# Two of 32 neighbour rows read as SBUF columns by ScalarE and VectorE in place of two POOL gathers

## The chip, the cores and the metric

The kernel runs on one core of one Trainium2 chip. The metric is device time in microseconds (us) of one execution. Before the change it is 36,141.66 us, the median of three runs (36,135.79 to 36,142.94). A core has five engines with queues of their own: TensorE (PE in the profile; its weight loads are PEld), VectorE (DVE), ScalarE (ACT), GpSimd (POOL) and SyncE (SP). Data lies in HBM, in SBUF (128 partitions) and in PSUM, where TensorE writes.

## The reference

A recommender: 50,001 items have 32 near items each, and 16,384 users have a history of 100 items and a target item. First every item gets two attention vectors over its 32 near items, one from `E_in` and one from `E_out` (32 numbers each). Then each user's history rows are scored against the target row.

```python
def _neighbor_attn(E, near_full):          # E: [50001, 32]
    V = E[near_full]                       # [50001, 32, 32]
    scores = einsum('nd,nkd->nk', E, V) / sqrt(32)
    w = softmax(scores, axis=-1)
    return einsum('nk,nkd->nd', w, V)
a_sus = _neighbor_attn(E_in, near_full);  a_inf = _neighbor_attn(E_out, near_full)
h = concat([E_hist[history], a_sus[history], a_inf[history]])   # [B, 100, 128]
t = concat([E_tgt[target], a_inf[target], a_sus[target]])       # [B, 128]
z = relu(einsum('bld,hd->blh', h * t[:, None, :], W1) + b1)
exp_A = exp(einsum('blh,h->bl', z, W2[0])) * mask
attn = exp_A / sum(exp_A) ** 0.5
s = sum(h * attn);  out = sigmoid(cosine(s broadcast, t))
```

All arithmetic is float32. The indices are random, so neighbour rows and history rows lie anywhere in their tables.

## The kernel before

It has two stages, one after the other.

The **item stage** (lines 91 to 164) makes two tables in HBM, `table` and `ttab`, one row of 128 numbers per item. `egeo` in HBM holds for each item its `E_in` row and its `E_out` row side by side, 64 numbers or 256 bytes. The items, padded to 50,048, are cut into 23 blocks (`it`) of 128 partitions by 17 (`j`). One pair (it, j), 128 items, one per partition, is called a **sub-step** here; there are 391. SP loads each block's neighbour numbers `nidx`, its own rows `own` and the history embeddings into `row` (lines 101 to 107). In a sub-step POOL issues 32 indirect DMAs (line 111), one per neighbour k: each fetches 128 rows of `egeo`, one per partition, into `v[:, k]`. VectorE multiplies `v` by the own row, which ScalarE has copied to PSUM (lines 118 and 120), sums over the 32 numbers of each half (line 127), takes the maximum over the neighbours (lines 129 and 130); ScalarE makes the exponentials and their sums (line 134); VectorE takes the reciprocal (line 142), weights `v` (line 145, once per half), sums over the neighbours (line 152) and scales into `row` (line 153). ScalarE copies the two halves swapped into `trow` (line 160). At a block's end SP stores `row` and `trow` (lines 163 and 164). At the very start ScalarE's queue issues a copy of the target embeddings from HBM to HBM into `ttab` (lines 91 and 92).

Tiles come from pools with a fixed number of buffers. `v` has five, so POOL can be up to five sub-steps ahead of the engine that reads it; `prod` and `wv` have two. The order of instructions on each engine is made by the framework's scheduler from the program; waits between engines are semaphores that it places.

The **user stage** (lines 167 to 292) gathers history rows of `table` with 12,800 indirect DMAs on POOL (line 233) and target rows with 128 more (line 197), turns each on TensorE (line 246), multiplies by the target row (line 248), and runs the two matrix products (lines 255 and 265) with a ReLU between (line 257). It can begin only when the tables are complete in HBM. The last lines (295 to 325) reduce to the output.

Of the kernel before, what the change touches and what calls it, by code (L numbers as in the profile page):

```python
# [9 lines left out]

F32 = mybir.dt.float32
I32 = mybir.dt.int32
AF = mybir.ActivationFunctionType
ALU = mybir.AluOpType
AX = mybir.AxisListType

P = 128
ITEMS = 50001
K = 32
G = 32  # L20
DE = 64
D = 128
# [7 lines left out]
NSUB = 17  # L30
NITER = -(-ITEMS // (P * NSUB))
ROWS = NITER * P * NSUB

# [7 lines left out]
def kernel(  # L43
# [11 lines left out]
    out: bass.AP,  # L55
):
    nc = tc.nc

    const = ctx.enter_context(tc.tile_pool(name="const", bufs=1))
    dram = ctx.enter_context(tc.tile_pool(name="dram", bufs=1, space=bass.MemoryType.DRAM))  # L60


    table = dram.tile([ROWS, D], F32, name="table")

    ttab = dram.tile([ROWS, D], F32, name="ttab")

    ident = const.tile([P, P], F32, name="ident")
# [16 lines left out]
    scale = 1.0 / math.sqrt(G)  # L84
    near_v = near.rearrange("(i p j) k -> i p j k", p=P, j=NSUB)
    egeo_v = egeo.rearrange("(i p j) d -> i p j d", p=P, j=NSUB)
    ehist_v = ehist.rearrange("(i p j) d -> i p j d", p=P, j=NSUB)
    table_v = table.rearrange("(i p j) d -> i p j d", p=P, j=NSUB)
    ttab_v = ttab.rearrange("(i p j) d -> i p j d", p=P, j=NSUB)

    nc.scalar.dma_start(ttab[0 : ITEMS - 1, 0:DE], etgt[0 : ITEMS - 1, :])
    nc.scalar.dma_start(ttab[ITEMS - 1 : ITEMS, 0:DE], etgt[ITEMS - 1 : ITEMS, :])
    with (
        tc.tile_pool(name="n_in", bufs=2) as n_in,
        tc.tile_pool(name="n_v", bufs=5) as n_v,
        tc.tile_pool(name="n_p", bufs=2) as n_p,
        tc.tile_pool(name="n_s", bufs=3) as n_s,
        tc.tile_pool(name="n_ps", bufs=2, space=bass.MemoryType.PSUM) as n_ps,
    ):
        for it in range(NITER):  # L100
            nidx = n_in.tile([P, NSUB, K], I32, name="nidx")
            nc.sync.dma_start(nidx, near_v[it])
            own = n_in.tile([P, NSUB, 2 * G], F32, name="own")
            nc.sync.dma_start(own, egeo_v[it])
            row = n_in.tile([P, NSUB, D], F32, name="row")
            nc.sync.dma_start(row[:, :, 0:DE], ehist_v[it])
            trow = n_in.tile([P, NSUB, 2 * G], F32, name="trow")
            for j in range(NSUB):
                v = n_v.tile([P, K, 2, G], F32, name="v")
                for k in range(K):  # L110
                    nc.gpsimd.indirect_dma_start(  # L111
                        out=v[:, k].rearrange("p t d -> p (t d)"),
                        out_offset=None,
                        in_=egeo,
                        in_offset=bass.IndirectOffsetOnAxis(ap=nidx[:, j, k : k + 1], axis=0),
                    )
                own_ps = n_ps.tile([P, 1, 2 * G], F32, name="own_ps")
                nc.scalar.copy(own_ps[:, 0, :], own[:, j, :])  # L118
                prod = n_p.tile([P, K, 2, G], F32, name="prod")
                nc.vector.tensor_tensor(  # L120
                    prod.rearrange("p k t d -> p k (t d)"),
                    v.rearrange("p k t d -> p k (t d)"),
                    own_ps.to_broadcast([P, K, 2 * G]),
                    ALU.mult,
                )
                sc = n_s.tile([P, 2, K], F32, name="sc")
                nc.vector.tensor_reduce(sc.rearrange("p t k -> p k t"), prod, AX.X, ALU.add)  # L127
                top = n_s.tile([P, 2], F32, name="top")
                nc.vector.tensor_reduce(top, sc, AX.X, ALU.max)
                nc.vector.tensor_scalar(top, top, -scale, None, ALU.mult)  # L130
                ex = n_ps.tile([P, 2, K], F32, name="ex")
                tot = n_s.tile([P, 2, 1], F32, name="tot")
                for t in range(2):
                    nc.scalar.activation(  # L134
                        ex[:, t, :],
                        sc[:, t, :],
                        AF.Exp,
                        bias=top[:, t : t + 1],
                        scale=scale,
                        accum_out=tot[:, t, :],  # L140
                    )
                nc.vector.reciprocal(tot, tot)  # L142
                wv = n_p.tile([P, 2, G, K], F32, name="wv")
                for t in range(2):
                    nc.vector.tensor_tensor(  # L145
                        wv[:, t].rearrange("p d k -> p k d"),
                        v[:, :, t, :],
                        ex[:, t, :].rearrange("p (k o) -> p k o", o=1).to_broadcast([P, K, G]),
                        ALU.mult,
                    )  # L150
                att = n_s.tile([P, 2, G], F32, name="att")
                nc.vector.tensor_reduce(att, wv, AX.X, ALU.add)  # L152
                nc.vector.tensor_tensor(  # L153
                    row[:, j, DE:D].rearrange("p (t d) -> p t d", t=2),
                    att,
                    tot.to_broadcast([P, 2, G]),
                    ALU.mult,
                )
                for t in range(2):
                    nc.scalar.copy(  # L160
                        trow[:, j, t * G : (t + 1) * G], row[:, j, D - (t + 1) * G : D - t * G]
                    )
            nc.sync.dma_start(table_v[it], row)
            nc.sync.dma_start(ttab_v[it][:, :, DE:D], trow)


    num = const.tile([P, UC], F32, name="num")
# [3 lines left out]
    hist_v = history.rearrange("(p i j) l -> i p j l", p=P, j=BSUB)  # L171
    tidx = const.tile([P, UC], I32, name="tidx")
    nc.scalar.dma_start(tidx, target.rearrange("(p c) -> p c", p=P))
    tidf = const.tile([P, UC], F32, name="tidf")
    nc.vector.tensor_copy(tidf, tidx)
    with (
# [12 lines left out]
        def target_rows(c):  # L189

            if c % BSUB == 0:
                hidx = u_in.tile([P, BSUB, L], I32, name="hidx")
                nc.sync.dma_start(hidx, hist_v[c // BSUB])
# [11 lines left out]
        def target_work(c):  # L205
# [8 lines left out]
            junk = u_t.tile([P, D], F32, name="junk")  # L214
            nc.scalar.activation(junk, t, AF.Square, accum_out=tsq[:, c : c + 1])
            idf = u_s.tile([P, L], F32, name="idf")
# [11 lines left out]
        def gather(c, g):  # L228
            u = users[c]
            h = u_h.tile([P, LG, D], F32, name="h")  # L230
            for q in range(LG):
                l = g * LG + q
                nc.gpsimd.indirect_dma_start(  # L233
                    out=h[:, q, :],
                    out_offset=None,
                    in_=table,
                    in_offset=bass.IndirectOffsetOnAxis(ap=u["hidx"][:, l : l + 1], axis=0),
                )
            u["h", g] = h

        def turn(c, g):
            u = users[c]
            h = u.pop(("h", g))
            hT_ps = ps_t.tile([P, LG, P], F32, name="hT_ps")
            for q in range(LG):
                nc.tensor.transpose(hT_ps[:, q, :], h[:, q, :], ident)  # L246
            xT = u_x.tile([D, LG, P], F32, name="xT")
            nc.vector.tensor_tensor(xT, hT_ps, u["tT"].to_broadcast([D, LG, P]), ALU.mult)  # L248
            nc.vector.tensor_reduce(u["hsum"][:, g * LG : (g + 1) * LG], h, AX.X, ALU.add)  # L249
            u["xT"][g] = xT  # L250

        def hidden(c, g):
# [3 lines left out]
            z = u_x.tile([HID, LG, P], F32, name="z")  # L256
            nc.scalar.activation(z, z_ps, AF.Relu, bias=b1_sb)  # L257
            u["z"][g] = z

        def scored(c, g):  # L260
# [9 lines left out]
            ea = u_s.tile([P, L], F32, name="ea")  # L270
            nc.scalar.activation(ea, u["score"], AF.Exp)
            nc.vector.tensor_tensor(ea, ea, u["keep"], ALU.mult)
# [7 lines left out]
        for s in range(len(groups) + 2):  # L280
            if s < len(groups):
                c, g = groups[s]
# [12 lines left out]
    with (  # L295
# [3 lines left out]
        root = f_s.tile([P, UC], F32, name="root")  # L299
        nc.scalar.activation(root, den, AF.Sqrt)  # L300
        part = f_s.tile([P, UC], F32, name="part")
# [6 lines left out]
        s = f_s.tile([P, 1], F32, name="s")  # L308
# [4 lines left out]
        nc.vector.tensor_scalar(n1, n1, float(D), EPS * EPS, ALU.mult, ALU.max)  # L313
        nc.scalar.activation(n1, n1, AF.Sqrt)
        n2 = f_s.tile([P, UC], F32, name="n2")
# [65 lines left out]
```

## Time and profile before

| what | value |
|---|---|
| timed runs, median of 3 | 36,141.66 us |
| the profiled execution, its own time | 31,810.23 us |
| its span, first to last instruction | 31,808.5 us |
| last stores of the item stage issued | at 15,641 us |
| POOL busy | 24,005.7 us (75%), in 25,446 instructions |
| TensorE (PE) busy | 15,238.9 us (48%), nearly all in the user stage |
| VectorE (DVE) busy | 8,951.2 us (28%) |
| ScalarE (ACT) busy | 2,851.2 us (9%) |
| mean granted TensorE clock | 0.752 |

The profile is of one execution, and this one was 4,331 us shorter than the median of the timed runs. Register, branch and semaphore instructions, and those that only issue a DMA from SP or ScalarE, are not counted as busy; an indirect DMA on POOL is. In a row of the groups the fields are: line, engine, operation, output and input with their shapes, count, busy time in us, mean duration of one in ns, then the engine's idle time just before these instructions and what ended it; "issue" means that nothing in the profile ended it. A row of the timeline has the start in us, the duration in us, then the same names, and in brackets the idle time before it.

### The profile page before, as it was taken

To read this page: it belongs to the slowest core of one execution; us is meant where nothing else is said; L and a number is where in the kernel's file an instruction comes from. 1 tells how busy PE (TensorE), PEld (TensorE's weight loads), DVE (VectorE), ACT (ScalarE), POOL (GpSimd) and SP (SyncE) were. 2 spreads that over 40 slices of the span, in tenths; PEclk is the share of its full clock that TensorE was granted. 3 is DMA by queue.
4 is the path that set the end of the run, shared out by engine and by line. 5 is a ranking of instruction groups with operands and counts; after the bars stand their busy time and mean duration, and the time that the engine had idled before them with its cause. 6 is when DMAs were issued, how large, how long until landed. Compare 5 with 4: busy or idle time off the path is not lost.

```text
span 31808.5 us, 154035 instructions
## 1 busy us (share of the span) xinstructions
PE 15238.9 (48%) x44931; PEld 9632.2 (30%) x44931; DVE 8951.2 (28%) x10957; ACT 2851.2 (9%) x6458; POOL 24005.7 (75%) x25446
## 2 busy tenths in 40 slices
PE   0000000000000000000299999999999999999999
PEld 0000000000000000000155555555555555555555
DVE  2222222222222222222222222222222222222222
ACT  0000000000000000000011111111111111111111
POOL 7777777777777777777777777777777777777777
PEclk9999999999999999999955555555555555555555
DMA  2111111111111111111122222222222222222221
GB/s 50 30 30 30 30 31 33 30 30 30 30 34 30 30 30 30 31 33 28 37 54 53 54 53 54 53 54 54 53 54 53 54 53 54 54 53 54 53 54 52
DMA packets 981064, 1358.75 MB, mean 43 GB/s; under 512 B 559872, under 2 KB 564352, under 8 KB 977280
## 3 DMA queue, kind: packets, MB, share of 16 engines
q0 software_dynamic: 814080, 1258.87, 17.1%
q1 hardware_dynamic: 115952, 77.16, 0.9%
q10 hardware_dynamic: 50192, 12.87, 0.2%
q8 instruction: 363, 5.95, 0.1%
q14 instruction: 477, 3.91, 0.0%
HBM read 1308.76 MB, written 51.30 MB: 43 GB/s over the span
## 4 chain that ended last, share of the span: by engine, by line
POOL 49%; issue 19%; PE 15%; DMA 14%; DVE 2%; ACT 1%; POOLq 0%; ACTq 0%; SPq 0%; DVEq 0%
POOL v L111 35%; POOL h L233 13%; DMA h<-table,hidx 11%; PE z_ps L255 7%; PE score L265 5%; PE hT_ps L246 3%; DMA v<-in_egeo_dram,nidx 2%; DVE xT L248 2%; ACT z L257 1%; POOL t L197 0%; POOLq L233 0%; DVE tT L211 0%; DVE ea L274 0%; DMA nidx<-in_near_dram 0%; DMA ttab<-trow 0%
## 5 line engine op out<-in xcount | busy, mean ns | idle before, releaser
L233 POOL DMA_INDIRECT h<-table,hidx x12800 | 12079.2, 944 | 3900.9 <-issue 3159.2
L111 POOL DMA_INDIRECT v<-in_egeo_dram,nidx x12512 | 11805.1, 943 | 3820.9 <-issue 3719.2
L209 PE MATMUL hT_ps<-ident,t 128*128 128x128 f32 x128 | 53.9, 421 | 15644.7 <-DMA t<-ttab,tidx 15644.7
L265 PEld LDWEIGHTS score<-w_sb,z 128*128 128x128 f32 x25600 | 6225.7, 334 | 1080.8 <-ACT z L257 1074.0
L255 PE MATMUL z_ps<-xT,w1T 128*128 128x512 f32 x6400 | 6526.7, 1123 | 0.0
L265 PE MATMUL score<-w_sb,z 128*128 128x1 f32 x25600 | 5903.9, 335 | 235.4 <-ACT z L257 150.2
L246 PE MATMUL hT_ps<-ident,h 128*128 128x128 f32 x12800 | 4715.0, 439 | 673.3 <-DMA h<-table,hidx 520.3
L249 DVE TENSOR_REDUCE hsum<-h 128x4 f32<-128x512 f32 x3200 | 2194.7, 686 | 9243.7 <-DMA h<-table,hidx 9226.9
L209 PEld LDWEIGHTS hT_ps<-ident,t 128*128 128x128 f32 x128 | 28.8, 225 | 15644.9 <-ACT idf L217 15644.9
L246 PEld LDWEIGHTS hT_ps<-ident,h 128*128 128x128 f32 x12800 | 2676.6, 209 | 5434.3 <-issue 3257.2
L120 DVE TENSOR_TENSOR prod<-v,own_ps 128x2048 f32<-128x2048 f32 x391 | 894.6, 2288 | 10794.7 <-DMA v<-in_egeo_dram,nidx 10794.4
L257 ACT ACTIVATE z<-z_ps,b_sb 128x512 f32<-128x512 f32 x3200 | 2199.1, 687 | 13448.3 <-PE z_ps L255 13335.1
L248 DVE TENSOR_TENSOR xT<-hT_ps,tT 128x512 f32<-128x512 f32 x3200 | 2210.2, 691 | 2028.6 <-PE hT_ps L246 2026.8
L255 PEld LDWEIGHTS z_ps<-xT,w1T 128*128 128x128 f32 x6400 | 1745.4, 332 | 0.0
L145 DVE TENSOR_TENSOR wv<-v,ex 128x1024 f32<-128x1024 f32 x782 | 1398.8, 1867 | 0.0
L118 ACT COPY own_ps<-own 128x64 f32<-128x64 f32 x391 | 84.4, 216 | 11499.9 <-DVE prod L120 11498.4
L127 DVE TENSOR_REDUCE sc<-prod 128x64 f32<-128x2048 f32 x391 | 894.5, 2288 | 13.4
L152 DVE TENSOR_REDUCE att<-wv 128x64 f32<-128x2048 f32 x391 | 893.8, 2286 | 13.4
L160 ACT COPY trow<-row 128x32 f32<-128x32 f32 x782 | 131.7, 215 | 2465.7 <-DVE row L153 2465.7
L134 ACT ACTIVATE ex<-sc,top 128x32 f32<-128x32 f32 x782 | 227.7, 291 | 1081.9 <-DVE top L130 1069.2
L142 DVE RECIPROCAL tot<-tot 128x2 f32<-128x2 f32 x391 | 64.8, 166 | 362.3 <-ACT ex L134 362.3
L197 POOL DMA_INDIRECT t<-ttab,tidx x128 | 120.7, 943 | 60.5 <-issue 60.5
(49 smaller groups left out, 808.6 us busy)
## 6 DMA issues: line engine op xcount, KB each, us to landing
h<-table,hidx POOLq DMA_INDIRECT x12800, 2.5
v<-in_egeo_dram,nidx POOLq DMA_INDIRECT x12512, 2.4
table<-row SPq DMA_DIRECT2D x23, 1088.0 KB, 4.4
own<-in_egeo_dram SPq DMA_DIRECT2D x23, 544.0 KB, 3.6
row<-in_ehist_dram SPq DMA_DIRECT2D x23, 544.0 KB, 6.7
ttab<-trow SPq DMA_DIRECT2D x23, 544.0 KB, 6.8
ttab<-in_etgt_dram ACTq DMA_DIRECT2D x1, 12500.0 KB, 53.5
hidx<-in_history_dram SPq DMA_DIRECT2D x32, 200.0 KB, 2.5
```

The source lines that it names most:

```text
L111: nc.gpsimd.indirect_dma_start(out=v[:, k].rearrange("p t d -> p (t d)"), out_offset=None, in_=egeo, in_offset=bass.IndirectOffsetOnAxis(a ...
L120: nc.vector.tensor_tensor(prod.rearrange("p k t d -> p k (t d)"), v.rearrange("p k t d -> p k (t d)"), own_ps.to_broadcast([P, K, 2 * G]), ...
L127: nc.vector.tensor_reduce(sc.rearrange("p t k -> p k t"), prod, AX.X, ALU.add)
L145: nc.vector.tensor_tensor(wv[:, t].rearrange("p d k -> p k d"), v[:, :, t, :], ex[:, t, :].rearrange("p (k o) -> p k o", o=1).to_broadcast ...
L152: nc.vector.tensor_reduce(att, wv, AX.X, ALU.add)
L233: nc.gpsimd.indirect_dma_start(out=h[:, q, :], out_offset=None, in_=table, in_offset=bass.IndirectOffsetOnAxis(ap=u["hidx"][:, l : l + 1], ...
L246: nc.tensor.transpose(hT_ps[:, q, :], h[:, q, :], ident)
L248: nc.vector.tensor_tensor(xT, hT_ps, u["tT"].to_broadcast([D, LG, P]), ALU.mult)
L249: nc.vector.tensor_reduce(u["hsum"][:, g * LG : (g + 1) * LG], h, AX.X, ALU.add)
L255: nc.tensor.matmul(z_ps, w1T, u["xT"].pop(g), start=True, stop=True)
L257: nc.scalar.activation(z, z_ps, AF.Relu, bias=b1_sb)
L265: nc.tensor.matmul(u["score"][:, l : l + 1], z[:, q, :], w2_sb, start=True, stop=True)
```

## The change

In the item stage two of the 32 neighbours of each item no longer come by an indirect DMA. The `egeo` table is also held in SBUF, transposed: two items (64 numbers each) make a column of 128 numbers, one per partition, so `geoT` is 128 partitions by 25,024 columns of float32. A neighbour's two-item column is then a slice of four bytes in every partition, at an address that depends on the neighbour's number.

- **Building `geoT`** (`transposed`): 66 loads by SP of up to 384 column rows, three TensorE transposes each, and one ScalarE copy each from PSUM into `geoT`.
- **Addresses** (in `load`, once per block of 17 sub-steps): VectorE turns the last two neighbour numbers into byte addresses of columns, as floats; TensorE transposes them so that the 128 addresses of one neighbour of a sub-step lie in one row of `cols`; `odd` keeps which of the two items in the column is meant.
- **Columns** (`registers` and `columns`): an engine loads 32 addresses from `cols` into 32 of its registers with one instruction and then copies 32 columns, one instruction each, from `geoT` into the tile `g`. `AUX = ("AAAA", "DDDD")` says that ScalarE does all four blocks of 32 for one neighbour and VectorE all four for the other. For each sub-step that is four register loads and 128 copies on each of the two engines.
- **Back** (`turn`, `even`, `odd_half`): TensorE transposes the two tiles `g` into PSUM; ScalarE copies the first item of each column into `v[:, 30:32]`, and VectorE overwrites those for which `odd` is set with the second item.
- **POOL** issues 30 indirect DMAs a sub-step. `SPNUM, SPDEN = 0, 1` leaves the branch in which SP would fetch a neighbour unused.
- **Order**: the item stage's instructions on PE, ScalarE, VectorE and SP stand in the order of the program text (`manual_schedule`), as a pipeline three sub-steps deep. In step s, POOL gathers sub-step s, the column copies for s are spread in eight slots between the work on s - 1 (products, scores, exponentials) and s - 2 (weighted sums), and s - 3 is finished. `prod` and `wv` now have one buffer; `g` has two; `v` still has five.
- The stores of a block's rows (line 163 and 164 before) are issued from ScalarE's queue.

The user stage's text is the same.

```diff
+AUX = ("AAAA", "DDDD",)
+NAUX = len(AUX)
+SPNUM, SPDEN = 0, 1
+NREG = 32
+PAIRS = ROWS // 2
+NST = 3
...
+    geoT = nc.alloc_sbuf_tensor("geoT", (P, PAIRS), F32).ap()
+    geoT_at = nc.sbuf_base - 4 * PAIRS
+    geoT_b = geoT.bitcast(U8)
...
+        tc.manual_schedule(engines={E.PE, E.Activation, E.DVE, E.SP}),
+        tc.tile_pool(name="n_st", bufs=2) as n_st,
...
-        tc.tile_pool(name="n_p", bufs=2) as n_p,
+        tc.tile_pool(name="n_p", bufs=1) as n_p,
+        tc.tile_pool(name="n_g", bufs=2) as n_g,
...
+            colf = n_p.tile([P, NSUB, NAUX + 1], F32, name="colf")
+            coli = n_p.tile([P, NSUB, NAUX], I32, name="coli")
+            aux = nidx[:, :, K - NAUX : K]
+            nc.vector.tensor_scalar(coli, aux, 1, None, ALU.logical_shift_right)
+            nc.vector.tensor_copy(colf[:, :, 1 : NAUX + 1], coli)
+            nc.vector.tensor_scalar(colf[:, :, 1 : NAUX + 1], colf[:, :, 1 : NAUX + 1],
+                4.0, float(geoT_at), ALU.mult, ALU.add)
...
+            nc.tensor.transpose(col_ps[0:n, 0, :], colf.rearrange("p j a -> p (j a)"), ident)
+            cols = n_in.tile([n, P], I32, name="cols")
+            nc.vector.tensor_copy(cols, col_ps[0:n, 0, :])
...
+        def registers(s, a, engine, i0, low, top):
+            it, j = divmod(s, NSUB)
+            r = j * (NAUX + 1) + a
+            _, vals = nc.values_load_multi_w_load_instructions(
+                its[it][5][r : r + 1, i0 : i0 + NREG],
+                engines=[engine],
...
+        def columns(s, a, i0):
+            e = AUX[a][i0 // NREG]
+            vals = registers(s, a + 1, ENGINE[e], i0, geoT_at, geoT_at + 4 * (PAIRS - 1))
+            g = subs[s]["g"][a].bitcast(U8)
+            copy = nc.scalar.copy if e == "A" else nc.vector.tensor_copy
+            for i in range(i0, i0 + NREG):
+                copy(g[:, 4 * i : 4 * i + 4], geoT_b[:, ds(vals[i - i0] - geoT_at, 4)])
...
+        def turn(s):
+            back = n_pt.tile([P, 4, P], F32, name="pt")
+            for a in range(NAUX):
+                nc.tensor.transpose(back[:, a, :], subs[s]["g"][a], ident)
...
+        for s in range(NT + 3):
+            if s < NT:
+                if s % NSUB == NSUB // 2 and s // NSUB + 1 < NITER:
+                    load(s // NSUB + 1)
+                gather(s)
+            one, two, three = (0 <= s - d < NT for d in (1, 2, 3))
+            work = [
+                lambda: one and turn(s - 1),
+                lambda: (two and weighted(s - 2, 0), one and even(s - 1)),
+                lambda: two and weighted(s - 2, 1),
+                lambda: one and (odd_half(s - 1), products(s - 1)),
+                lambda: one and scores(s - 1),
+                lambda: two and attend(s - 2),
+                lambda: three and finish(s - 3),
+                lambda: one and exponents(s - 1),
+            ]
+            for w in range(len(work)):
+                work[w]()
+                if s < NT:
+                    for blocks in (acts, dves):
+                        n = len(blocks)
+                        for c in blocks[-(-w * n // 8) : -(-(w + 1) * n // 8)]:
+                            columns(s, *c)
```

## The prediction

> **What bounds the kernel now.** I read the page first, then the timeline of a stretch in the middle of the item stage, then the timeline of the hand-over to the user stage and of the first 14 us. The page's head, two rows of its busy slices, the chain and the groups of the item stage:
>
> ```profile
> span 31808.5 us, 154035 instructions
> ...
> PE   0000000000000000000299999999999999999999
> ...
> POOL 7777777777777777777777777777777777777777
> ...
> POOL v L111 35%; POOL h L233 13%; DMA h<-table,hidx 11%; PE z_ps L255 7%; PE score L265 5%; PE hT_ps L246 3%; DMA v<-in_egeo_dram,nidx 2%; DVE xT L248 2%; ACT z L257 1%; POOL t L197 0%; POOLq L233 0%; DVE tT L211 0%; DVE ea L274 0%; DMA nidx<-in_near_dram 0%; DMA ttab<-trow 0%
> ...
> L111 POOL DMA_INDIRECT v<-in_egeo_dram,nidx x12512 | 11805.1, 943 | 3820.9 <-issue 3719.2
> ...
> L120 DVE TENSOR_TENSOR prod<-v,own_ps 128x2048 f32<-128x2048 f32 x391 | 894.6, 2288 | 10794.7 <-DMA v<-in_egeo_dram,nidx 10794.4
> ```
>
> POOL is busy to the same seven tenths in every slice; the rest of its time is "issue", a gap of 0.30 us in which it waits for nothing the profile shows. So a gather costs (11805.1 + 3820.9) / 12512 = 1.249 us on POOL, and 32 of them make the 40.0 us of a sub-step (128 items; 391 of them). VectorE waits 10794 us for gathers. The timeline shows the metronome, and what VectorE and ScalarE do in between:
>
> ```profile
> 5009.04 0.94 POOL L111 DMA_INDIRECT v<-in_egeo_dram,nidx  x1 [0.30 <-issue]
> 5009.07 0.17 DVE L130 TENSOR_SCALAR top<-top 128x2 f32<-128x2 f32 x1
> ...
> 5010.17 0.17 DVE L142 RECIPROCAL tot<-tot 128x2 f32<-128x2 f32 x1 [0.93 <-ACT ex L134]
> 5010.25 3.58 DVE L145 TENSOR_TENSOR wv<-v,ex 128x1024 f32<-128x1024 f32 x2
> 5010.28 0.94 POOL L111 DMA_INDIRECT v<-in_egeo_dram,nidx  x1 [0.30 <-issue]
> ...
> 5016.44 0.34 ACT L160 COPY trow<-row 128x32 f32<-128x32 f32 x2 [6.31 <-DVE row L153]
> ```
>
> The item stage ends at 15641 us, when the last rows go to HBM; the user stage fills the other 16,160 us at the same 1.248 us a gather, with TensorE above 90% busy beside it. The built instruction streams of the user stage are the same in both kernels, engine by engine, so I leave it alone.
>
> **The two times of before.** The profiled execution took 31,810 us, the median of the timed runs is 36,142, 13.6% more. The profile cannot say where the 4,332 us lie: a gather may take 1.42 us in a timed run, or the user stage may be held by TensorE. I make the sum against 31,810, subtract the difference from 36,142, and keep the scaled saving for the low end.
>
> [...] The new VectorE copies go SBUF to SBUF with an even count[...]: L130, such an instruction, takes 168 ns at least and 187 in the mean, with up to 245 where it begins within 50 ns before a gather starts; POOL's spacing stays 1.248 us around it. [...] 10.17 to 10.25 above is 80 ns from start to start, and the two ScalarE copies of L160 (215 ns each alone) take 0.34 us together, so the second comes 125 ns after the first, of which some 25 are its 28 further elements. [...] No load of registers is in the trace of before.
>
> **The change, part by part.**
>
> Removed: 2 of 32 gathers a sub-step. 391 x 2 x 1.249 = 977 us, as POOL is the pace. The new sub-step is 30 x 1.249 = 37.5 us, and this is now the time in which each of the two other engines must do its share.
>
> ScalarE, per sub-step: 4 register loads (32 registers each), 128 column copies of 4 bytes per partition, one more copy out of PSUM (some 0.28 us, by the nearest row, L160 with 215 ns at 32 elements). Its own work stays: own_ps 0.22, the two exponentials 0.87 from first to last, trow 0.34; with the new copy 1.7 us. A column copy lies between 0.10 us (overlapped) and 0.19 (its whole duration); I take 0.10, 12.8 us. [...] I take 2.0[...]: 8.0 us. Sum 22.5 us, 15 below the pace.
>
> VectorE: own work from the rows L120, L127, L129, L130, L142, L145, L152, L153: 2.29 + 2.29 + 0.22 + 0.19 + 0.17 + 3.58 + 2.29 + 0.23 = 11.3 us, plus the predicated copy of 128x128 out of PSUM, 0.35 by the 322 ns of the three-operand instruction L220. Column copies between 0.08 and 0.166 us (L142 whole); I take 0.10: 12.8 us. Four loads at 2.0: 8.0 us. Sum 32.5 us: hidden, but with only 5 us to spare. Without that cover each further microsecond is paid 391 times. Both engines run in written order, so a load that blocks the sequencer holds up every copy and every reduction behind it; on VectorE the products, scores and weighted sums queue behind it, and POOL waits for these when its five v buffers are full.
>
> TensorE: two transposes a sub-step and one per 17, 0.45 us each, on an engine idle in this stage: nothing. The small integer preparation of addresses, 6 VectorE instructions and a copy per 17 sub-steps, about 1.5 us x 23 = 35 us in all, lies in VectorE's spare time; uncovered it would be those 35. The table stores move from SP's queue to ScalarE's, 0.33 + 0.56 us of issue per 17 sub-steps, in its spare time. SP's loads of the next 17 sub-steps are issued half-way through the present ones and stand behind nothing but the start-up loads. Instruction fetch grows: the two instruction queues moved 9.86 MB for 154,035 instructions, 64 bytes each, so 264 more are 17 KB a sub-step, on DMA engines busy 15% in this stage: nothing. The longer pipeline (three sub-steps) ends with the same chain as before, plus 0.6 us.
>
> Start-up: 66 loads of up to 196 KB, 196 transposes and 66 ScalarE copies build the transposed table before the first column can be read. ScalarE's queue is first held by the issue of the target-table copy:
>
> ```profile
> 1.39 50.72 ACTq L92 DMA_DIRECT2D ttab<-in_etgt_dram  x1
> ```
>
> So the chain starts in earnest at about 53 us. Two load buffers: a load of about 3 us (own, 544 KB, lands in 3.6) and three transposes (1.4 us) per buffer, two at a time, 2.3 us apiece: 66 x 2.3 = 150, done at about 205 us. Then sub-step 0's columns (21 us), sub-step 1 (27), and 8 us into sub-step 2 the first v buffer is free: 261 us. POOL, from 9.7 us on, has filled five buffers at 9.7 + 5 x 37.5 = 197 us. It stalls 64 us. Bounds: 15 us at 1.6 us per piece, 140 at 3.5.
>
> [...] at 0.10 us a copy the four bursts last 12.8 us and run beside 10 of the 30 gathers. Below: nothing, as around L130. Above: 0.2 us for each, 2.0 us a sub-step (once, at 15652, POOL's gap is 0.50 instead of 0.30 beside such an instruction). I take 0.05 us x 10 = 0.5 us: 391 x 0.5 = 195 us. The range keeps 0 and 780.
>
> Sum: 31,810 - 977 + 64 + 195 = 31,092, 718 us less. From the median: 36,142 - 718 = 35,424; I forecast 35,420 us.
>
> **The rivals.**
>
> VectorE becomes the bound, slower than before. Its sub-step passes the old 40.0 us when 4 loads take over 40.0 - 11.65 - 12.8 = 15.6 us, so from 3.9 us a load (122 ns a register) on. At 5 us the sub-step is 44.5, 391 x 4.5 = 1,760 us more, with start-up 37,970. [...] For: [...] copies at loaded addresses whose sequencer time the trace does not show. [...]
>
> Contention eats the gain: at 0.25 us on each of the 10 gathers, or 0.083 on all 30, 2.5 us a sub-step are back and the time is 36,142 plus 64. For: [...] the one long gap; against: L130's neighbours, undisturbed.
>
> The saving is scaled: if a gather takes 1.42 us in the timed runs, 782 x 1.42 = 1,110 us go, the other engines have 42.6 us, and with little contention the time is 35,080.
>
> **How the numbers follow.** Forecast 0.42, scaled saving 0.20, contention 0.11, VectorE bound 0.27. What a measurement of this kernel can tell is about 0.2%, 72 us. Faster: the first two, and a little of the contention case, 0.64; within: most of the contention case, 0.06; slower: 0.30. The low end is the scaled saving with a smaller start-up, 34,950. The high end goes into the VectorE case, to 4.6 us a load, 37,400, and leaves about 0.15 above it and 0.04 below. The likeliest case alone: 35,000 to 36,050.
>
> **What would show it.** Right: 30 gathers per sub-step at 1.25 to 1.28 us, the item stage ending near 14,920 us of the profiled execution, ScalarE and VectorE waiting for the gathers in every sub-step, one POOL stall before 300 us. VectorE bound: POOL waiting once per sub-step for the release of v, and VectorE's longest gaps at the register loads. Contention: POOL's spacing near 1.33 during the bursts. What would make it wrong beside these: a user stage that moves although its instructions are the same, since 4,332 us of the timed runs are unexplained.

## The result and the profile after

The changed kernel takes 38,648.35 us (median of four runs, 38,641.03 to 38,662.21), the kernel before 36,138.73 (four runs, 36,126.85 to 36,142.94). The ratio is 1.0695, interval 1.0682 to 1.0708: 2,510 us slower. The forecast was 35,420 and the top of its range 37,400.

The page of the changed kernel, its head, the chain and the groups that answer to those shown of before (the last two are the column copies):

```profile
span 38653.4 us, 262033 instructions
...
POOL 5555555555555555555556666666666666666666
...
PE 24%; another core or an unknown queue 16%; issue 4%; ACT 3%; DVE 1%; ACTq 0%; DMA 0%; DVEq 0%; POOL 0%; POOLq 0%
...
L215 POOL DMA_INDIRECT v<-in_egeo_dram,nidx x11730 | 11066.4, 943 | 8861.2 <-DVE wv L294 5394.2
...
L229 ACT COPY g<-geoT 128x4 uint8 x50048 | 5670.9, 190 | 9285.1 <-issue 8804.3
L229 DVE COPY g<-geoT 128x4 uint8 x50048 | 4645.7, 181 | 8335.7 <-issue 8098.1
```

A gather still lasts 943 ns, but POOL's row has gone from seven tenths to five, and POOL waits 5,394 us for VectorE's `wv`, that is, for a free `v` buffer. POOL has left the chain. ScalarE and VectorE now set the pace of the item stage, and they do it while idle: before their copies they wait 8,804 and 8,098 us for "issue", which is nothing that the profile shows. "Another core or an unknown queue" in the chain is time that the profile can put down to no instruction; this trace lacks many records (see what stays open).

The timeline of one sub-step of the changed kernel, where POOL restarts after its wait, and a stretch 13 us later:

```profile
5004.66 2.63 DVE L229 COPY g<-geoT 128x4 uint8 x32
5005.10 0.94 POOL L215 DMA_INDIRECT v<-in_egeo_dram,nidx  x1 [13.51 <-DVE wv L294]
...
5018.55 0.19 ACT L229 COPY g<-geoT 128x4 uint8 x1 [0.51 <-issue]
5018.55 0.17 DVE L229 COPY g<-geoT 128x4 uint8 x1 [0.53 <-issue]
5018.82 0.94 POOL L215 DMA_INDIRECT v<-in_egeo_dram,nidx  x1 [0.30 <-issue]
5019.25 0.19 ACT L229 COPY g<-geoT 128x4 uint8 x1 [0.51 <-issue]
5019.25 0.17 DVE L229 COPY g<-geoT 128x4 uint8 x1 [0.53 <-issue]
5019.95 0.19 ACT L229 COPY g<-geoT 128x4 uint8 x1 [0.50 <-issue]
...
5031.15 0.19 ACT L229 COPY g<-geoT 128x4 uint8 x1 [1.21 <-issue]
...
5032.55 0.19 ACT L229 COPY g<-geoT 128x4 uint8 x1 [1.21 <-issue]
```

At 5004.66 VectorE makes 32 copies in 2.63 us. From 5017 on, both engines start one copy at a time, at the same instants: 18.55, 19.25, 19.95; later ScalarE's start at 31.15 and 32.55. The steps are 0.70 us or a multiple of it. I call this the grid. It lasts until some 5 us after the sub-step's last gather (which starts at 5041.29), and the copies then flow again. Inside a block of 32 copies no other engine has anything to deliver: the registers are loaded (the next copy starts 0.08 us after a load's end on ScalarE, 0.09 on VectorE) and `geoT` is complete since 286 us. By start times in the whole trace, 6,435 of ScalarE's copies and 5,502 of VectorE's start 0.70, 1.40 or 2.10 us (each within 0.04) after the copy before; 99% of them lie between 3.6 and 42.2 us after the sub-step's first gather, whose last starts at 36.2.

### The profile page after: what moved, and what is told of

It reads as the page before. It is cut to its first block, busy times and chain, and to the rows that moved or that the text cites. A ratio compares the mean times of both kernels' runs of the same rounds, so it can differ in the third digit from the quotient of the medians.

```text
span 38653.4 us, 262033 instructions
## 1 busy us (share of the span) xinstructions
PE 14769.2 (38%) x45932; PEld 9639.1 (25%) x45932; DVE 13286.7 (34%) x61557; ACT 8584.7 (22%) x56963; POOL 23262.5 (60%) x24664
## 5 line engine op out<-in xcount | busy, mean ns | idle before, releaser
L215 POOL DMA_INDIRECT v<-in_egeo_dram,nidx x11730 | 11066.4, 943 | 8861.2 <-DVE wv L294 5394.2
L229 ACT COPY g<-geoT 128x4 uint8 x50048 | 5670.9, 190 | 9285.1 <-issue 8804.3
L229 DVE COPY g<-geoT 128x4 uint8 x50048 | 4645.7, 181 | 8335.7 <-issue 8098.1
L234 PE MATMUL pt<-ident,g 128*128 128x128 f32 x782 | 364.2, 472 | 18233.3 <-DVE g L229 12446.3
L460 PEld LDWEIGHTS score<-w_sb,z 128*128 128x128 f32 x25600 | 5925.4, 327 | 5409.0 <-ACT z L452 3971.5
L234 PEld LDWEIGHTS pt<-ident,g 128*128 128x128 f32 x782 | 141.7, 183 | 18451.8 <-DVE g L229 12554.3
L441 PEld LDWEIGHTS hT_ps<-ident,h 128*128 128x128 f32 x12800 | 3292.0, 261 | 3585.7 <-issue 3485.4
L441 PE MATMUL hT_ps<-ident,h 128*128 128x128 f32 x12800 | 4110.4, 424 | 6.8 <-DMA h<-table,hidx 4.7
L240 ACT COPY v<-pt 128x128 f32<-128x128 f32 x391 | 103.6, 265 | 3634.8 <-PE pt L234 3634.8
L310 DVE TENSOR_TENSOR row<-att,tot 128x64 f32<-128x64 f32 x391 | 88.3, 226 | 2019.3 <-remote 1141.0
L160 PE MATMUL pt<-ident,colf 128*51 128x128 f32 x23 | 9.8, 424 | 1175.1 <-DVE odd L157 1126.2
```

What stands on the lines that cost most here:

```text
L215: nc.gpsimd.indirect_dma_start(out=v[:, k].rearrange("p t d -> p (t d)"), out_offset=None, in_=egeo, in_offset=bass.IndirectOffsetOnAxis(a ...
L229: copy(g[:, 4 * i : 4 * i + 4], geoT_b[:, ds(vals[i - i0] - geoT_at, 4)])
L460: nc.tensor.matmul(u["score"][:, l : l + 1], z[:, q, :], w2_sb, start=True, stop=True)
```

## The experiments

**Where the 4,332 us of before are.** The profile that the prediction read was 31,810 us long, and the timed runs 36,142. So the kernel before was profiled again, unaltered.

> The kernel before, unchanged, profiled once more, to see where its timed runs (36,139 us) lose 4,330 us against its first profile (31,808 us). If ScalarE and VectorE also stall in ticks of 0.70 us here, as in the profile of the changed kernel: item stage near 15,640 us, because POOL is five buffers ahead there, and the user stage 18,500 to 20,500 us. If a gather itself is slower: spacing on POOL near 1.42 us in both stages. If the first profile was typical of profiles: 31,810 us again.

It took 36,276.74 us. Its page and its timeline in mid-stage:

```profile
span 36275.0 us, 154035 instructions
...
L111 POOL DMA_INDIRECT v<-in_egeo_dram,nidx x12512 | 13370.1, 1069 | 4124.2 <-issue 4018.5
```

```profile
5028.44 0.95 POOL L111 DMA_INDIRECT v<-in_egeo_dram,nidx  x1 [0.30 <-issue]
...
5031.07 1.10 POOL L111 DMA_INDIRECT v<-in_egeo_dram,nidx  x1 [0.30 <-issue]
5032.47 1.09 POOL L111 DMA_INDIRECT v<-in_egeo_dram,nidx  x1 [0.30 <-issue]
...
5036.67 1.79 POOL L111 DMA_INDIRECT v<-in_egeo_dram,nidx  x1 [0.30 <-issue]
5038.77 1.10 POOL L111 DMA_INDIRECT v<-in_egeo_dram,nidx  x1 [0.30 <-issue]
```

Here POOL is on the grid: gathers start 1.40 or 2.10 us apart for part of each sub-step, 1.25 elsewhere, and the mean gather is 1,069 ns instead of 943. The sub-step is 44.72 us instead of 39.93; over 391 that is 1,873 us. The user stage starts at 17,517 us instead of 15,649 and takes 18,758 us instead of 16,159. Both stages were slowed before the change, and the profile read for the prediction had none of it.

In the user stage the delay looks different. Of its 6,919 gathers between 20,000 and 30,000 us only 66 start 0.70, 1.40 or 2.10 us after the one before. There ScalarE, VectorE and POOL now and then stand for several microseconds and start again together (the product that the ScalarE line below reads was done at 25018.09):

```profile
25024.09 0.69 ACT L257 ACTIVATE z<-z_ps,b_sb 128x512 f32<-128x512 f32 x1 [9.94 <-remote]
25024.10 0.69 DVE L248 TENSOR_TENSOR xT<-hT_ps,tT 128x512 f32<-128x512 f32 x1 [8.68 <-remote]
25024.33 0.95 POOL L233 DMA_INDIRECT h<-table,hidx  x1 [3.33 <-remote]
```

"remote" says that the profile can name no instruction that ended the wait. Whether both delays have one cause is not shown.

Against this trace the changed kernel's item stage is 2,522 us longer (20,039 against 17,517) and its user stage 143 us shorter. This set of runs was 0.4% slower than the set of the result, and the 143 us belong to the set: the three kernels that follow were run in it and have user stages of 18,742 to 18,754 us. The whole loss is in the item stage.

**Which of the added instructions.** Three edits of the changed kernel, in the same set of runs.

```diff
-AUX = ("AAAA", "DDDD",)
+AUX = ("AAAA",)          # e2: ScalarE's neighbour alone, 31 gathers
+AUX = ("DDDD",)          # e3: VectorE's neighbour alone, 31 gathers
```

> Only ScalarE reads a neighbour as columns, POOL fetches 31 of 32. Theory A (the stalls come with the rate of instructions that ScalarE and VectorE together take in beside POOL's gathers): with half of the added instructions the stalls shrink to a third or less, POOL is the pace again, sub-step 38.7 us, item stage 15,200 us. Theory B (register loads and loaded addresses): the stalls per added instruction stay, ScalarE's sub-step is 40 to 48 us, item stage 15,700 to 18,800. Theory C (VectorE's copies and POOL block each other[...]): no stalls on ScalarE at all, 38.7 us.

> Only VectorE reads a neighbour as columns, POOL fetches 31 of 32. Theory A: stalls shrink to a third or less; VectorE 30 to 36 us, POOL the pace, sub-step 38.7 us, item stage 15,200 us. Theory B: VectorE stalls per added instruction as in the changed kernel, sub-step 44 to 50 us. Theory C: VectorE as in the changed kernel, sub-step 48 to 51 us, and ScalarE, which has no copies, is only late where it waits for VectorE.

e2 took 37,836 us with 48.1 us a sub-step, e3 38,401 with 49.5, against 50.5 for both together (50.9 in another set as slow as this one). Half the added instructions bring most of the delay, so it isn't proportional to them. ScalarE alone meets it too (in e2 it idles 9,327 us for "issue" before its copies, 8,804 with both), so VectorE's copies and POOL blocking each other isn't its cause.

```diff
-            vals = registers(s, a + 1, ENGINE[e], i0, geoT_at, geoT_at + 4 * (PAIRS - 1))
...
-                copy(g[:, 4 * i : 4 * i + 4], geoT_b[:, ds(vals[i - i0] - geoT_at, 4)])
+                copy(g[:, 4 * i : 4 * i + 4], geoT_b[:, 4 * (97 * i + 12000 * a) : 4 * (97 * i + 12000 * a) + 4])
```

> The changed kernel without its register loads: the same 256 copies per sub-step read columns at fixed addresses, so two of 32 neighbours are wrong ones. Theory A: the stalls stay, sub-step 46 to 50 us (50.7 less the loads, about 1 us each), item stage 18,000 to 19,700 us. Theory B: no stalls, POOL the pace at 37.5 us, item stage 14,750 us. Theory C: as A, 46 to 50 us.

e4 reads fixed columns (wrong neighbours) and took 38,209 us, 49.05 us a sub-step. Register loads and loaded addresses cost 1.5 to 1.9 us of a sub-step, by the set that it is compared with; the grid stays.

**The gathers beside the copies, and the count of copies.** Two edits of the changed kernel, and one memset of one column on POOL ahead of each sub-step's gathers in either kernel, to see whether the grid depends on how instructions fall together:

```diff
 # e5
-            for k in range(k1 if by_sp else k1 + 1):
-                nc.gpsimd.indirect_dma_start(...)
+            i0 = 128 * (s % 300)
+            nc.sync.dma_start(
+                v[:, 0 : k1 + 1].rearrange("p k t d -> p (k t d)"),
+                egeo[i0 : i0 + P * (k1 + 1), :].rearrange("(p k) d -> p (k d)", p=P),
+            )
 # e6: four adjacent columns at one loaded address, 8 registers a load
+            for i in range(i0, i0 + NREG, 4):
+                copy(g[:, 4 * i : 4 * i + 16], geoT_b[:, ds(vals[(i - i0) // 4] - geoT_at, 16)])
 # before_plus1, after_plus1
+                nc.gpsimd.memset(pad, 0.0)
```

> The changed kernel with POOL idle in the item stage: the 30 gathers of a sub-step are replaced by one contiguous load from SyncE of 30 rows per partition (so the neighbours are the wrong ones; the column copies, their register loads, and everything after stay). Theory G, ScalarE and VectorE are slowed to a grid of 0.70 us only while POOL's gathers are issued beside them: the sub-step falls from 50.7 us to what ScalarE's and VectorE's own instructions take when they flow, about 128 x 0.10 + 4 x 0.35 + 3.1 = 17 us on ScalarE and 128 x 0.075 + 4 x 0.4 + 12 = 23 us on VectorE, with the waits between them 25 to 33 us, and no copy starts 0.70 or 1.40 us after the one before. Rival, the copies slow themselves (two engines, each with 128 short instructions in a row): the gaps of 0.70 and 1.40 us stay and the sub-step stays at 45 to 51 us.

> The changed kernel with a quarter of the instructions: each copy moves four adjacent columns (16 bytes of each partition) at one loaded address, so a register load brings 8 registers and ScalarE and VectorE each issue 32 copies a sub-step instead of 128 (three of four items get the wrong neighbour). The gathers stay at 30. If the number of instructions sets the delay, the sub-step falls from 50.7 us to POOL's pace in this regime, which by the kernel before is 44.8 x 30/32 = 42.0 us, or to 37.5 us if POOL runs free. If the delay comes from the gathers and the work already there, and the copies only shift it, it stays above 44 us. The e2 run (half the copies, 48.0 us) speaks for something in between.

> The kernel before with one memset of one column on POOL ahead of each sub-step's gathers. By its work alone it costs 391 x 0.1 to 0.3 us = 40 to 120 us, in an item stage of 17,494 us. If POOL's waits on the grid of 0.70 us depend on how instructions fall together in groups rather than on their work, the item stage moves by several hundred microseconds, up or down (down to about 15,700 us at most, where there are none), with the memset's own cost inside it.

> The changed kernel with one memset of one column on POOL ahead of each sub-step's gathers. POOL waits 13.5 us in each sub-step for a free v buffer, so by its work the memset costs nothing: item stage 19,928 us within 60. If the delays depend on how instructions fall together in groups, the item stage moves by several hundred microseconds, up or down.

In this set the kernel before took 31,807 us; the set ran on another chip than e1 to e4. There was no grid in any of the four (one run each), so they say nothing of its cause; but they show what the change does without it. before_plus1 took 31,810 us: the memset costs nothing. The changed kernel with the same memset took 30,900 us, **907 us less than the kernel before on the same chip**. Its page:

```profile
span 30898.2 us, 262424 instructions
...
POOL 7777777777777777777777777777777777777777
...
POOL 52%; DMA 20%; issue 19%; PE 7%; DVE 1%; POOLq 0%; ACT 0%; ACTq 0%; SPq 0%; DVEq 0%
...
L218 POOL DMA_INDIRECT v<-in_egeo_dram,nidx x11730 | 11070.8, 944 | 3582.5 <-issue 3474.1
...
L232 ACT COPY g<-geoT 128x4 uint8 x50048 | 4919.1, 189 | 2150.4 <-issue 2149.2
L232 DVE COPY g<-geoT 128x4 uint8 x50048 | 3887.5, 194 | 2275.8 <-issue 2157.9
```

POOL is the pace again (its row is seven throughout, and it leads the chain), a sub-step's gathers take 37.45 us, and the "issue" idle before the copies is a quarter of what it was. What is left of it stands before blocks of 32 copies, where the registers are loaded, as the timeline of the same kernel shows:

```profile
5024.87 2.56 DVE L232 COPY g<-geoT 128x4 uint8 x32 [2.04 <-issue]
...
5025.36 3.14 ACT L232 COPY g<-geoT 128x4 uint8 x32 [1.64 <-issue]
```

e5 took 26,645 us with 26.35 us a sub-step: that is what the two engines need when nothing else holds them. e6 took 30,847 us.

**Is it the chip or the memset?** The changed kernel unaltered, and one with a third neighbour read as columns (`AUX = ("AAAA", "DDDD", "AADD",)`, 29 gathers):

> The changed kernel unaltered, timed against the kernel before once more. The kernel before took 36,280 us in one set of runs and 31,807 us in another, on another chip. If the delays on the 0.700 us grid belong to the chip on which a run falls and not to the kernels, the difference between the two kernels has two signs: where the kernel before takes about 31,810 us, the changed one takes 31,810 - 977 + start-up = about 30,900 us, ratio 0.971, and no copy waits on the grid; where the kernel before takes 36,100 to 36,300 us, the changed one takes about 38,650, ratio 1.07. If the padded memset of the earlier run was what freed the changed kernel, this run takes over 33,000 us also where the kernel before takes 31,810.

> The changed kernel with a third neighbour read as columns, half of it by ScalarE and half by VectorE: 29 gathers and 192 copies an engine in each sub-step. Without grid delays POOL stays the pace (VectorE about 11.65 + 192 x 0.075 + 6 x 0.4 = 28.5 us, ScalarE 1.7 + 192 x 0.097 + 6 x 0.35 = 22.4 us, against 36.2 us of gathers): a further 391 x 1.249 = 488 us go, about 30,410 us. With grid delays the two engines are the bound already and get half as many instructions again: between 54 and 62 us a sub-step, 39,900 to 43,000 us.

The kernel before took 36,285 us in this set, on a third chip, and the changed one 38,940: ratio 1.0731, interval 1.0713 to 1.0749. The third neighbour made it worse, 40,875 us (ratio 1.1264, interval 1.1245 to 1.1283), with 55.8 us a sub-step: more copies, more delay. It doesn't yet settle the question, since on this chip the kernel before meets the grid too.

**Do the delays need POOL's gathers?** e5 and e6 once more, with the other two:

> The changed kernel unaltered. On a chip where the kernel before takes 31,810 us: 31,810 - 977 + a start-up stall of 60 to 140 us = 30,890 to 30,970 us, no copy on the 0.700 us grid, POOL waiting for v only once, before 300 us. On a chip where it takes 36,100 to 36,300: 38,600 to 39,000 us, with the grid. If the padding of the run after_plus1 had made it fast, the first case gives over 33,000 us.

> The changed kernel with one contiguous load in place of the 30 gathers of a sub-step (wrong neighbours, all else kept). Where there is no grid it took 26,645 us, with 26.4 us a sub-step. Where there is: if ScalarE's and VectorE's delays need POOL's gathers beside them, the sub-step stays at 26 to 29 us and the whole, with a user stage of 18,700 us, takes 29,100 to 30,300 us; if their own instructions suffice for the delays, the sub-step is 36 us or more and the whole over 33,000 us.

> The changed kernel with copies of 16 bytes, a quarter as many (wrong neighbours for three of four items). Where there is no grid it took 30,847 us. Where there is: if the delay grows with the number of instructions, the sub-step lies between the 44.8 us of the kernel before (or 42.0, scaled to 30 gathers) and the 47.4 of half the copies; by a line through 50.7 us for 128 copies and 55.6 for 192 (4.9 us for 64), it is 50.7 - 7.3 = 43.4 us for 32 copies, and the whole takes 35,700 us. If the delay doesn't depend on the number, it stays near 50 us, 38,300 us.

> The changed kernel with a third neighbour read as columns. Where there is no grid: 29 gathers of 1.249 us = 36.2 us a sub-step, VectorE and ScalarE below it at about 28 and 22 us of their own, 30,400 us in all. Where there is: 40,870 us as before.

This set had the grid: before 36,136 us, the changed kernel 38,648, three columns 40,530. Without gathers the kernel took 29,083 us. Its copies, by the page:

```profile
L227 ACT COPY g<-geoT 128x4 uint8 x50048 | 4918.7, 189 | 2167.5 <-issue 2165.1
L227 DVE COPY g<-geoT 128x4 uint8 x50048 | 3705.6, 168 | 2296.9 <-issue 2181.7
```

The idle before them is 2,168 and 2,297 us, as on the chip without a grid (there it is 2,150 and 2,276 beside gathers), and a sub-step takes 26.35 us, equal on both chips. The same 256 copies on the same chip wait on the grid with gathers beside them, and don't without. The user stage of this run, which has gathers, is slowed as always (18,594 us). So on such a chip the grid needs the gathers; it isn't a limit of ScalarE or VectorE alone. The edit takes away with the gathers also their 32 DMA packets each and the records of their landings (below), so which part of a gather counts is not separated.

With a quarter of the copies the kernel took 35,305 us, 42.03 us a sub-step in the mean, close to the 43.4 that a line through the larger counts had given. But 25% of ScalarE's copies are on the grid there against 13% before: the grid is a condition that lasts for a time, and what an engine loses in it grows with the instructions that it has left to issue (sub-steps of 42.03, 50.5 and 55.3 us with 32, 128 and 192 copies an engine).

**How many gathers.** Half of them replaced by a contiguous load:

> The changed kernel unaltered. On a chip where the kernel before takes 31,810 us: 30,890 to 30,970 us, no copies on the 0.700 us grid; over 33,000 there if the padding of the run after_plus1 was what made that run fast. On a chip where the kernel before takes 36,100 to 36,300: 38,600 to 39,000 us.

> The changed kernel with 15 of the 30 gathers of a sub-step replaced by one contiguous load (wrong neighbours in these 15). Where there is no grid: VectorE's and ScalarE's own 26.4 us a sub-step, about 26,650 us. Where there is: if the delay is so much for each gather beside the copies, 26.5 us without gathers and 50.7 with 30 give 38.6 with 15, item stage about 15,300 and 33,900 us in all; if the delays only set in after some 8 gathers in a row, as in the changed kernel, fewer copies are hit and the sub-step is 27 to 33 us, 29,400 to 31,700 us in all.

> The changed kernel with one memset of one column on POOL ahead of each sub-step's gathers; it took 30,900 us on a chip without the grid. On one with it: 38,600 to 39,000 us as without the memset, if the delays follow the work; another item stage by several hundred microseconds, up or down, if they follow how instructions fall together in groups.

> The changed kernel with a third neighbour read as columns. Where there is no grid: 29 gathers of 1.249 us a sub-step, 30,400 us. Where there is: 40,500 to 40,900 us.

This set had the grid too: before 36,129 us, the changed kernel 38,641, three columns 40,516. With 15 gathers a sub-step takes 33.46 us (31,892 in all): 7.1 us more than with none, and the next 15 gathers add another 17.1. The delay is less than proportional at first, nearer to the reading in which a run of gathers must have gone out, and a little above its 33 us. With the memset the changed kernel took 38,653 us, 12 more than without: on this chip the padding neither makes nor removes the grid, so it isn't what made the 30,900 us. They belong to the other chip, or to that one set of runs: the chip without the grid was met in one set only, and the chip of the first trace of before, which has no grid either, is not on record. The chip of this set is that of e1 to e4, and had the grid both times, three hours apart, with 36,280 and 36,129 us for the kernel before; so the 0.4% between sets isn't a matter of the chip alone.

All together (us; sub-steps are mean distances between the products of one sub-step and the next):

| kernel | without grid: time, sub-step | with grid: time, sub-step |
|---|---|---|
| before | 31,807, 39.93 | 36,129 to 36,285, 44.72 |
| changed | 30,900 (with memset), 37.24 | 38,641 to 38,940, 50.5 to 50.9 |
| quarter of the copies | 30,847, 37.14 | 35,305, 42.03 |
| half of the gathers | not run | 31,892, 33.46 |
| no gathers | 26,645, 26.35 | 29,083, 26.35 |
| three columns | not run | 40,516 to 40,875, 55.3 to 55.8 |

No kernel that computes all neighbours was faster than the one before on a chip with the grid. The changed kernel without the memset was not run on a chip without it.

**What stays open** is what the grid is. One rival is the recording of the trace itself. In every trace with the grid most records of DMA landings, that is, of data that has arrived, are missing (a gather leaves 16 in a trace without it), so their pages give no time from issue to landing. The line of the first trace of before, and the same line of the second:

```profile
h<-table,hidx POOLq DMA_INDIRECT x12800, 2.5
```

```profile
h<-table,hidx POOLq DMA_INDIRECT x12800
```

The item stage of before has 202,128 such records in the first trace and 23,991 in the second; that of the changed kernel has 190,669 without the grid (with the memset) and 33,391 with it. Without gathers it has 9,248 on either kind of chip, and no grid. So records are lost where engines are delayed, and both need the gathers. Whether the recording holds the engines, or something else does both, no run shows: all executions on record come with a span and a granted clock, that is, were recorded in some way, and none was timed without. Records of the engines' own semaphores are missing too (1,783 of 4,335 are left in the item stage of before), so a wait named "issue" or "remote" in these traces can be another; the start times don't depend on that.

In the run without gathers ScalarE and VectorE issued the same copies with no grid in 26.35 us a sub-step, against 50.5 with gathers, so the records of these two engines alone aren't enough.

Slower fetching of instructions is not to be seen: between 300 and 14,000 us in the changed kernel the packets of 8 KB in the queue that fetches most of them take 438 ns in the mean with the grid and 431 without (with the memset). Why three chips had the grid and one had not was not found.

## Why the prediction was wrong

- **"The two times of before": this step failed.** It said that the profile couldn't tell where 4,332 us lie, took its saving of 718 us from the median, and so carried the 4,332 over as a constant: what the change does to them it put at nothing. They were no constant. In the second trace of before, 4,467 us longer than the first, 1,868 lie in the item stage, where POOL is on the grid, and 2,598 in the user stage. What is lost in the item stage depends on which engine has short instructions to issue while gathers run. The change put 256 of them on ScalarE and VectorE, and this loss grew by some 3,250 us (worked out below). The overlap failed with it: 22.5 and 32.5 us of work were to be hidden behind 37.5 us of gathers; the sub-step took 50.5.
- **The sum itself holds where there is no grid.** 31,810 - 977 + 64 is 30,897, and the changed kernel with its memset took 30,900, one run. That the two meet within 3 us is in part luck (next point). The 195 us that the prediction put on POOL for copies beside gathers were not there: POOL's spacing stays 1.249 us while copies flow. VectorE's copies show 194 ns in the mean beside gathers (with the memset) and 168 without gathers.
- **Start-up.** Predicted: table done at 205 us, POOL stalled for 64. Without grid: 173 and 63. With it: 286 and 132. That 63 meets 64 is luck: the table was done 32 us sooner than predicted, and POOL went on 87 us after that, not 56.
- **ScalarE and VectorE.** The register loads of 32 take 1.98 us on ScalarE and 2.15 on VectorE (medians in the changed kernel). The 2.0 of the prediction was my estimate: the trace of before holds no such load. Copies that flow start 0.095 us apart on ScalarE and 0.071 on VectorE (medians in the changed kernel), predicted 0.10. The 25 ns that the prediction counted for L160's 28 further elements is the difference between L160's 215 ns and the 190 of ScalarE's copies of four bytes. Without gathers the sub-step is 26.35 us, VectorE's, predicted 32.5. "Hidden, but with only 5 us to spare" was too careful without the grid.
- **With the grid, by the steps.** The sub-step rises from 37.45 to 50.54 us (13.09), that of before from 39.94 to 44.72 (4.78). The change adds 13.09 - 4.78 = 8.31 us of grid to each, 3,249 us in all. It saves 974 on gathers, loses 132 at start-up, and 88 at the end, where the user stage's first gather follows the last of the item stage after 111 us instead of 23. That is the other engines' arrears, not the longer pipeline: without the grid it is 24 in the changed kernel. Sum 2,495, against 2,522 between the two item stages.
- **The rivals.** "VectorE becomes the bound" got the place right: POOL waits once per sub-step for the release of `v`. Its mechanism was wrong, since it needed 3.9 us a load where VectorE's take 2.15. Contention on POOL and the scaled saving fall: in the changed kernel POOL's gathers keep 1.249 us with the grid as well, and POOL isn't the bound there. Two ends of the range were summed a little off: the scaled saving gives 36,142 - 1,110 + 64 = 35,096, not 35,080, and 4.6 us a load gives some 37,300, not 37,400; nothing hangs on either.
- **"A user stage that moves although its instructions are the same"** was named as what would make it wrong. It is 2,430 to 2,620 us longer with the grid than without, but within one set of runs nearly the same for all kernels. The item stage was slowed too, and there the change met it.

## What to carry to other kernels

When the profiled execution and the timed runs differ by 13%, take a second profile that has the time of the timed runs before making a sum; the difference has a place, and a change can make it larger. See whether its page still gives the times from issue to landing: where they are gone, records are missing. Spare time on an engine isn't spare for many short instructions if something makes it issue one per 0.70 or 1.40 us for more than half of each sub-step, as here from 5017 to 5047 us: count instructions, not only microseconds, on the engines that are to take over work beside indirect DMAs. Compare kernels on one chip and in one set of runs, and say whether the grid was there: here the sign of the change went with it.

## What the runs showed of the hardware that I had not expected

- The same kernel takes 31,807 us on one chip and 36,129 to 36,285 on three others. On these, while POOL issues the item stage's gathers, instructions of ScalarE, VectorE or POOL start only at steps of 0.70 us for part of the time, and most records of DMA landings are missing (23,991 of 202,128 in the item stage of before).
- Which engine is held differs with the kernel: POOL in the kernel before (gathers 1.40 or 2.10 us apart), ScalarE and VectorE in the changed one, in the same ticks, with POOL beside them at its 1.249 us.
- A load of 32 registers from SBUF takes 1.98 us on ScalarE and 2.15 on VectorE, and one of 8 registers 0.55 and 0.61, about 62 to 76 ns a register. Four adjacent columns at one loaded address cost as many instructions as one.
